# Variances of the second half of the tokens moved to ScalarE inside the query stage, with three sums moved

## The chip, the cores and the metric

The kernel runs on one core of a Trainium2 chip. A core has engines that run beside each other, each with its own in-order queue of instructions: TensorE (PE, matrix products into the eight PSUM banks), VectorE (DVE), ScalarE (ACT), GpSimd (POOL) and SyncE (SP), whose queue here only issues DMAs. Sixteen DMA engines move data between HBM and the on-chip SBUF. The metric is the device time of one execution in microseconds (us), as the median over several runs: 1160.79 us before the change (three runs, 1159.8 to 1162.68).

## What is computed

One transformer block in float32 on 16 sequences of 128 tokens with 1024 features each:

```python
x = x + xattn(_layernorm(x), ctx, ctx, w_q, w_k, w_v, w_out, mask)   # 32 query heads, 8 key/value groups
x = x + ffn(_layernorm(x), w12, b12, w3, b3)                         # (silu(x1) * x2) @ w3.T + b3

def _layernorm(x, axis=-1, eps=1e-05):
    m = jnp.mean(x, axis=axis, keepdims=True)
    v = jnp.var(x, axis=axis, keepdims=True)
    return (x - m) / jnp.sqrt(v + eps)
```

In the attention, `query = q @ w_q.T`, the scores are `query . key / sqrt(32)`, masked, put through a softmax and multiplied with the values. The change concerns the first layer norm only, and in it only the per-token variance.

## The kernel before

**How the first layer norm is folded away.** Queries are linear in the normalised x. The mean is removed from the weights instead of the tokens (`centre`, L442), so the query product runs on raw x. The factor 1/sqrt(var + eps) of each token is applied later, to the scores, as the per-partition number `rstd` of the instruction at L760. It is kept in `mr[T][:, 1, t]`: T = 0 for the sequences 0 to 7 (the first half) and T = 1 for 8 to 15. These numbers must be there before the first score row of the half is scaled, and for nothing else.

**How the variances are made.** For the first half `q_squares` (L622) does it on ScalarE inside the query stage: one pass over the 128x1024 tile `xs` sums it (L626), a tiny one makes minus the mean (L627), one more sums the squared deviations (L628). After the eighth sequence a GpSimd instruction divides by 1024 and `inv_std` (L213) turns eight variances into eight factors: seven tiny instructions on GpSimd and ScalarE. For the second half `q_stats` (L617) does it on VectorE with `mean_var` (L205): two `bn_stats` of 128x512, one `bn_aggr`, one copy of two numbers, for each of eight sequences. It is called from `hook` in `seven_round` (L727), along with the load of the tile, while keys and values of the second half are made.

**Products by seven.** Large matrix products are done with Strassen-like schemes (`seven`, L272): seven block products in place of eight, with sums of input blocks on the left and right made beforehand and sums of results made afterwards. The query product has two levels: outer products (g, i) with i from 1 to 7 for two halves g of the weights are the 14 entries of `Q_STEPS`, and each step runs seven inner products in the order 1, 5, 6, 7, 2, 3, 4. One inner product is four matrix passes, one step 28 passes, about 12 us. In a step, product 1 fills a PSUM bank, ScalarE copies it out (`p1`, L284), VectorE adds `u1` (L287) and `u3` (L290), and products 2, 3 and 4 go on accumulating into the banks of 1, 5 and 7. So product 3 waits until `u3` has read its bank.

**What the steps read.** Left sums of weights (`QI`, `q_inner_left`, L542) are made on GpSimd, four per step. Right sums of x come in two layers: outer sums (`q_outer_right`, L488), made mostly on GpSimd, in place, in tiles named `xq` and `Y`; inner sums (`q_inner_right`, L501), always on VectorE, in tiles `Y_T` (`Y7_T6` is inner sum 6 of outer product 7).

**What sets the order.** `q_at((n, j), ...)` puts a function into a plan that is called right after inner product number j of step n (`q_follow`). In steps 0 to 9 every engine's queue is written out in this order by hand. `q_plans` (L633) holds the plan. Steps 10 to 13, the seven-product rounds for keys and values of the second half (`seven_round(1, k)`) and the first output round run as filler between the attention instructions of the first eight sequences; TensorE's order is by hand there, and a scheduler orders the other engines at build time by the position of the code and the readiness of operands. The filler's left sums for keys (`sums_left7(1, 0)`, L693) are eight GpSimd subtractions and additions; `ctx_sum` (L695) makes right sums of the context on VectorE or GpSimd.

**Buffers.** Nearly all large tiles come from one pool of 44 units of 512 KB (`NUNIT`). A tile that is allocated takes a unit that became free, and its first writer waits for the last users of that unit. Loads are issued from the one SP queue in program order; a load that waits for its unit holds up everything behind it.

**Attention.** `scores` (L743) does, for one sequence and half of the heads, 16 score products, then VectorE scales and masks (L760) and finds the maximum (L763), ScalarE does the exponentials (L769), VectorE a reciprocal (L775), GpSimd the scaling (L778). The four score banks become free only when the exponentials have read them. `turn_V` (L422) transposes values on TensorE into a bank, `flip` (L781) transposes probabilities.

Of the kernel before, what the change touches and what calls it, by code (L numbers as in the profile page):

```python
# [13 lines left out]
AF = mybir.ActivationFunctionType  # L14
ALU = mybir.AluOpType
# [5 lines left out]
D = 1024  # L21
# [10 lines left out]
NT = B // 2  # L32
# [96 lines left out]
def xattn_ffn_kernel(  # L129
# [33 lines left out]
    nc = tc.nc  # L163
# [11 lines left out]
    def temp(shape, name):  # L175
        return temps.tile([P, *shape], F32, tag="tmp", name=name)
# [14 lines left out]
    def load(src, shape, name, eng=nc.sync):  # L191
        t = unit(shape, name)
        eng.dma_start(t, src)
        return t
# [10 lines left out]
    def mean_var(xt, dst, name):  # L205
        st = small.tile([P, 2, nc.vector.BN_STATS_DIM], F32, tag="st", name=f"st_{name}")
        for h in range(2):
            nc.vector.bn_stats(st[:, h, :], xt[:, ts(h, 512)])
        mv = small.tile([P, 2], F32, tag="mv", name=f"mv_{name}")
        nc.vector.bn_aggr(mv, st)  # L210
        nc.vector.tensor_copy(dst, mv)

    def inv_std(mr, name):  # L213

        n = mr.shape[2]
        v, t = (small.tile([P, NT], F32, tag=f"inv_std{i}", name=f"is{i}_{name}", bufs=2)[:, :n] for i in range(2))
        y = mr[:, 1, :]
        nc.gpsimd.tensor_scalar(v, y, EPS, None, ALU.add)
        nc.scalar.activation(t, v, AF.Ln)
        nc.scalar.activation(y, t, AF.Exp, scale=-0.5)  # L220
        nc.gpsimd.tensor_mul(t, y, y)
        nc.gpsimd.tensor_mul(t, t, v)
        nc.gpsimd.tensor_scalar(t, t, -0.5, 1.5, ALU.mult, ALU.add)
        nc.gpsimd.tensor_mul(y, y, t)
# [177 lines left out]
    mr = [const.tile([P, 2, NT], F32, tag=f"mr{T}", name=f"mr_{T}") for T in range(2)]  # L402
    later, xs = [], {}

    def soon(n, gen):

        later.append([n, gen])

    def tick():
        for item in list(later):  # L410
            item[0] -= 1
            if item[0] <= 0:
                later.remove(item)
                stream.work.appendleft(item[1])

    def load_xs(t):
        xs[t] = load(x[t], [D], f"xs_{t}")

    def stats(t):
        mean_var(xs.pop(t), mr[t // NT][:, :, t % NT], f"a{t}")  # L420

    def turn_V(T, c, r, t):  # L422

        pt = bank(f"vt_{T}_{c}_{r}").rearrange("p (t k) -> p t k", t=4)
        for i in range(4):
            nc.tensor.transpose(pt[:, i, :], t[:, ts(i, S)], ident)  # L426
            yield 0.17
        if (T, c) not in V:
            V[T, c] = unit([4, KV], f"V_{T}_{c}")
        nc.scalar.copy(V[T, c][:, :, ts(r, P)], pt)  # L430

    def key_home(T, c, r):
        if (T, c) not in KT:
            KT[T, c] = unit([GH, 512], f"K_{T}_{c}")
        return KT[T, c][:, r, :]
# [36 lines left out]
    def q_at(n, j, fn, *args):  # L472
        qplan.setdefault((n, j), []).append((fn, args))
# [140 lines left out]
            *((INNER,) if n < AHEAD else ((1, 6, 5, 7, 2, 3, 4), nc.vector.tensor_copy)),  # L614
        )

    def q_stats(t):  # L617
        stats(t)
        if t % NT == NT - 1:
            inv_std(mr[t // NT], f"a{t // NT}")  # L620

    def q_squares(t):  # L622

        xt = xs.pop(t)
        less = mr[0][:, 0, t : t + 1]
        nc.scalar.activation(xt, xt, AF.Identity, accum_out=less)  # L626
        nc.scalar.mul(less, less, -1.0 / D)  # L627
        nc.scalar.activation(xt, xt, AF.Square, bias=less, accum_out=mr[0][:, 1, t : t + 1])  # L628
        if t == NT - 1:
            nc.gpsimd.tensor_scalar(mr[0][:, 1, :], mr[0][:, 1, :], 1.0 / D, None, ALU.mult)  # L630
            inv_std(mr[0], "a0")

    def q_plans():  # L633
        for n, (g, i) in enumerate(Q_STEPS):
            if i > 2:
                q_at(n - 2, 3, q_load_left, g, i)
            for e, k in enumerate((1, 5, 6, 7, 3)):
                q_at(n - 1, 3 + e if n else min(5 + e // 2, 7), q_inner_left, g, i, k)
            if i in (1, 2, 5, 3):
                q_at(n - 1, 6 if n else 7, q_hold, g, i)  # L640
            if i == 1:
                q_at(g - 1, 7, q_keep_left, g, 4)
                q_at(g - 1, 7, q_outer_left, g)
                q_at(g, 7, q_keep_left, g, 3, 6)
                q_at(g + 1, 2, q_keep_left, g, 5, 7)
                q_at(n + 1, 2, q_store, g, i, "U")
            if i == 2:
                q_at(n + 1, 2, q_gather, g, 2, "U")
                q_at(n + 2, 3, q_final, g, 2, 0, 0)
            if i == 6:  # L650
                q_at(n - 2, 4, q_fetch, g, "U")
                q_at(n + 1, 2, q_store, g, "u", "V")
            if i == 7:
                q_at(n + 1, 2, q_store, g, "u", "W")
            if i == 4:
                q_at(n, 7, q_stay, g, "u", 1)
            if i == 5:
                q_at(n + 1, 3, q_gather, g, "V", 5)
                q_at(n + 1, 3, q_gather, g, "W", 5)
                q_at(n + 1, 4, q_given, g, "W", 1)  # L660
            if i == 3:
                q_at(*((n + 1, 3) if g == 0 else (n, 7)), q_gather, g, "V", 3)
                q_at(n, 7, q_given, g, "V", 0)
        for e, (K, C) in enumerate(((0, 0), (1, 0), (1, 1), (0, 1))):
            for f, (h, c) in enumerate(((0, 0), (0, 1), (1, 1), (1, 0))):
                when = ((-1, 3 + (f + 1) // 2), (0, 1 + f), (0, 5 + f // 2), (1, 2 + f))[e]
                q_at(*when, load_xq, K, C, h, c)
        for i, hcs, ks in (
            (1, [(-1, 5)] * 4, ((-1, 6), (-1, 6), (-1, 7), (0, 1))),
            (2, [(0, 6)] * 4, ((0, 7), (1, 1), (1, 2), (1, 7))),  # L670
            (5, [(2, 1), (2, 2), (2, 7), (3, 1)], ((8, 7), (9, 1), (9, 2), (9, 7))),
            (6, [(2, 7), (3, 1), (3, 3), (3, 3)], ((3, 5), (3, 6), (3, 7), (4, 1))),
            (7, [(4, 5), (5, 1), (5, 2), (5, 5)], ((5, 2), (5, 7), (6, 1), (6, 2))),
            (4, [(6, 5), (7, 1), (7, 2), (7, 5)], ((7, 2), (7, 7), (8, 1), (8, 2))),
            (3, [(4, 4)] * 4, ((4, 4), (5, 4), (8, 4), (8, 6))),
        ):
            for when, hc in zip(hcs, ((0, 0), (0, 1), (1, 1), (1, 0))):
                q_at(*when, q_outer_right, i, *hc)
            for when, k in zip(ks, (5, 6, 7, 4)):
                q_at(*when, q_inner_right, i, k)  # L680
        for t in range(NT):
            q_at(t + 1, 1, load_xs, t)
            q_at(t + 2, 2, q_squares, t)
        for m in (0, 1, 4, 5):
            q_at(8, 1 + m, q_home, 0, m)
        q_at(11, 3, load_left7, 1)
        for j, e in ((1, 0), (1, 5), (2, 1), (4, 3)):
            q_at(12, j, lambda e=e: ctx_work[1][e][1]())
        for when, i, e in (
            ((12, 6), 5, 0), ((12, 7), 5, 1), ((13, 2), 6, 0), ((13, 4), 6, 1), ((13, 5), 7, 0), ((13, 7), 7, 1),  # L690
        ):
            q_at(*when, ctx_sum, i, e)
        q_at(13, 3, sums_left7, 1, 0)  # L693

    def ctx_sum(i, e):  # L695

# [19 lines left out]
    def seven_round(T, k, R):  # L716
        def done(rc, s, ps):
            r, c = rc
            dst = temp([512], f"vT_{T}_{c}_{r}") if k else key_home(T, c, r)
            if s is None:  # L720
                nc.scalar.copy(dst, ps)
            else:
                nc.vector.tensor_add(dst, s, ps)
            if k:
                soon(3, turn_V(T, c, r, dst))

        def hook(j):  # L727
            tick()
            if (T, k, j) == (1, 0, 4):
                sums_left7(1, 1)  # L730
            if (T, k) == (1, 0) and j < 3:
                ctx_sum(4, j - 1)
            if T == 1 and j < 5:
                load_xs(NT + 4 * k + j - 1)
            if T == 1 and j > 2 and j < 7:
                q_stats(NT + 4 * k + j - 3)
            transition(T, k, j)

        yield from seven(left7.pop((T, k)), R, f"Q7_{T}_{k}", done, hook, (1, 2, 5, 6, 7, 3, 4))
# [249 lines left out]
    with tc.manual_schedule(engines={ENGINES.PE, ENGINES.DVE}):  # L989
        q_plans()  # L990
        Feed(ctx_work[0][:6], 100)
        sums_left7(0, 0, 1)
        stream.add(in_turn(seven_round(0, 0, ctx_R[0]), seven_round(0, 1, ctx_R[0]), 1))
        stream.finish()
# [4 lines left out]
    for T in range(2):  # L999
# [8 lines left out]
        for i in range(NT * GH):  # L1008
            t, gh = T * NT + i // GH, i % GH
# [333 lines left out]
    for t in range(8, B):  # L1343
        n, j = divmod(t - 8, 2)
# [68 lines left out]
```

## Time and profile before

The profile is that of one execution, by the hardware profiler.

| what | value |
|---|---|
| median of three runs | 1160.79 us |
| the profiled execution's own time | 1162.42 us |
| its span (first to last instruction) | 1160.6 us |
| mean granted TensorE clock | 0.997 of full |
| busy: PE / DVE / ACT / POOL | 98% / 73% / 34% / 56% of the span |
| one 512 KB load of an x tile (`xs`), issue to landing | 3.9 / 6.8 / 11.1 us (least, median, most of 16) |
| query stage, steps 0 to 9 | about 60 to 182 us |
| attention, first eight sequences | about 182 to 345 us |

How to read it: busy time says which engine has no slack; here that is TensorE. What it loses is then found as its idle stretches, each of which the profile gives with the instruction that ended it ("idle before <- releaser"), and in the granted clock, which is a share of full speed. Idle time of any other engine matters only where it ends in one of these stretches. Line numbers are those of the kernel before; in the kernel after, the lines from L422 on are 3 lower, those of `q_squares` 8 and then 7 lower, those from L695 on 5 lower, and those from L743 on 9 lower.

### The profile page before, as it was taken

To read this page: it belongs to the slowest core of one execution; us is meant where nothing else is said; L and a number is where in the kernel's file an instruction comes from. 1 tells how busy PE (TensorE), PEld (TensorE's weight loads), DVE (VectorE), ACT (ScalarE), POOL (GpSimd) and SP (SyncE) were. 2 spreads that over 40 slices of the span, in tenths; PEclk is the share of its full clock that TensorE was granted. 3 is DMA by queue.
4 is the path that set the end of the run, shared out by engine and by line. 5 is a ranking of instruction groups with operands and counts; after the bars stand their busy time and mean duration, and the time that the engine had idled before them with its cause. 6 is when DMAs were issued, how large, how long until landed. Compare 5 with 4: busy or idle time off the path is not lost.

```text
span 1160.6 us, 13625 instructions
## 1 busy us (share of the span) xinstructions
PE 1141.1 (98%) x4232; PEld 534.2 (46%) x4232; DVE 848.8 (73%) x1179; ACT 395.4 (34%) x1429; POOL 653.0 (56%) x591
## 2 busy tenths in 40 slices
PE   9999999999989999999999999999999999999998
PEld 4444444445445554545454544444444444444443
DVE  4577988798977778778546456757777887979772
ACT  1222223657557576666361321210011022111211
POOL 5669935786567456547533359822523342648465
PEclk9999999999989999999999999999999999999999
DMA  9699674954254330332584889858734878282511
GB/s 364 251 368 348 227 265 144 211 154 153 91 200 181 128 128 37 128 128 91 200 306 165 315 334 326 237 199 259 176 121 159 212 197 272 91 270 82 173 73 73
DMA packets 70233, 227.42 MB, mean 196 GB/s; under 512 B 7824, under 2 KB 7824, under 8 KB 70160
## 3 DMA queue, kind: packets, MB, share of 16 engines
q1 hardware_dynamic: 62672, 199.81, 46.7%
q0 software_dynamic: 6624, 24.12, 11.2%
q10 hardware_dynamic: 864, 2.62, 0.6%
q8 instruction: 34, 0.56, 0.2%
q14 instruction: 39, 0.32, 0.1%
HBM read 139.49 MB, written 79.69 MB: 189 GB/s over the span
## 4 chain that ended last, share of the span: by engine, by line
PE 91%; DVE 4%; ACT 2%; issue 1%; DMA 1%; POOL 1%; SPq 0%; ACTq 0%; POOLq 0%; DVEq 0%
PE F_b L199 28%; PE Q_b L199 21%; PE O_b L199 15%; PE G_b L199 15%; PE pt L784 4%; PE s L751 3%; PE o L799 2%; ACT p L769 2%; PE xt L899 1%; DVE ctx_T L700 1%; DVE s L760 0%; DVE xnT L1066 0%; DVE Y_T L509 0%; DMA xnr<-xn_dram 0%; PE vt L426 0%
## 5 line engine op out<-in xcount | busy, mean ns | idle before, releaser
L769 ACT ACTIVATE p<-s,nmax 128x128 f32<-128x128 f32 x512 | 181.8, 406 | 125.7 <-DVE nmax L763 114.8
L778 POOL TENSOR_TENSOR p<-p,inv 128x512 f32<-128x512 f32 x128 | 136.4, 1098 | 138.4 <-DVE inv L775 121.1
L199 PE MATMUL F_b<-X_T,L 128*128 128x512 f32 x304 | 135.7, 592 | 0.0
L769 ACT ACTIVATION_READ_ACCUMULATOR p<-s,nmax 128x1 f32 x512 | 125.5, 245 | 0.0
L199 PE MATMUL G_b<-w_R,A_L 128*128 128x512 f32 x256 | 114.5, 592 | 0.0
L760 DVE SCALAR_TENSOR_TENSOR s<-s,mr,drop 128x512 f32<-128x512 f32 x128 | 90.3, 750 | 28.8 <-PE s L751 28.6
L784 PEld LDWEIGHTS pt<-ident,p 128*128 128x128 f32 x512 | 63.6, 142 | 70.0 <-issue 63.5
L199 PEld LDWEIGHTS F_b<-X_T,L 128*128 128x128 f32 x304 | 57.4, 190 | 70.8 <-issue 68.6
L763 DVE TENSOR_REDUCE nmax<-s 128x4 f32<-128x512 f32 x128 | 81.7, 679 | 0.0
L284 ACT COPY F_p<-F_b 128x512 f32<-128x512 f32 x28 | 16.4, 586 | 188.3 <-PE F_b L199 188.3
L784 PE MATMUL pt<-ident,p 128*128 128x128 f32 x512 | 77.3, 274 | 1.5 <-issue 1.5
L303 POOL TENSOR_TENSOR x<-x,G_n 128x512 f32<-128x512 f32 x36 | 52.8, 1491 | 46.3 <-DVE G_n L366 29.4
L384 ACT COPY G_c<-G_b 128x512 f32<-128x512 f32 x52 | 30.5, 586 | 140.7 <-PE G_b L199 137.3
L199 PEld LDWEIGHTS G_b<-w_R,A_L 128*128 128x128 f32 x256 | 48.6, 190 | 61.3 <-issue 59.3
L1176 DVE TENSOR_TENSOR M<-F_u,F_b 128x512 f32<-128x512 f32 x57 | 39.0, 685 | 46.3 <-PE F_b L199 42.8
L303 POOL TENSOR_TENSOR x<-x,G_c 128x512 f32<-128x512 f32 x36 | 54.8, 1538 | 31.9 <-DMA x<-x_dram 13.0
L199 PE MATMUL Q_b<-Y_T,QI 128*128 128x512 f32 x136 | 62.4, 594 | 1.9 <-DVE Y_T L509 1.9
L199 PE MATMUL O_b<-wo_T,O_S 128*128 128x512 f32 x128 | 63.3, 603 | 0.0
L199 PE MATMUL O_b<-wo,O_S 128*128 128x512 f32 x128 | 62.5, 602 | 0.0
L199 PE MATMUL F_b<-xnT,L 128*128 128x512 f32 x128 | 60.9, 593 | 0.0
L199 PE MATMUL O_b<-wo,OTr 128*128 128x512 f32 x112 | 56.0, 603 | 0.0
L287 DVE TENSOR_TENSOR F_u<-F_b,F_p 128x512 f32<-128x512 f32 x28 | 19.3, 691 | 45.2 <-PE F_b L199 41.5
(244 smaller groups left out, 2265.9 us busy)
## 6 DMA issues: line engine op xcount, KB each, us to landing
w<-in_w_dram SPq DMA_DIRECT2D x36, 512.0 KB, 6.3
xq<-in_xT_dram SPq DMA_DIRECT2D x16, 512.0 KB, 9.8
xs<-in_x_dram SPq DMA_DIRECT2D x16, 512.0 KB, 6.8
xp<-in_x_dram SPq DMA_DIRECT2D x16, 512.0 KB, 6.6
x_dram<-xp SPq DMA_DIRECT2D x16, 512.0 KB, 2.8
xn_dram<-xn SPq DMA_DIRECT2D x16, 512.0 KB, 2.9
xnr<-xn_dram SPq DMA_DIRECT2D x16, 512.0 KB, 5.7
h<-hT_dram SPq DMA_DIRECT2D x16, 512.0 KB, 6.0
```

The source lines that it names most:

```text
L199: nc.tensor.matmul(ps, lhsT, rhs, start=start and i == 0, stop=stop and i == len(pairs) - 1, skip_group_check=True,)
L287: nc.vector.tensor_add(u1, banks[6], p1)
L303: (eng.tensor_add if op == "+" else eng.tensor_sub)(out, a, b)
L384: nc.scalar.copy(t, ps)
L751: nc.tensor.matmul(ps[gl][:, j, :], QT[T, gh * HPG + j][rows, c, toks], KT[T, c][rows, gh, toks], start=True, stop=True,)
L760: nc.vector.scalar_tensor_tensor(s, s, rstd, drop.unsqueeze(1).to_broadcast([P, HPG, S]), ALU.mult, ALU.add,)
L763: nc.vector.tensor_reduce(nmax[:, e], s, AX.X, ALU.max, negate=True)
L769: nc.scalar.activation(p[:, j, :], ps[gl][:, j, :], AF.Exp, bias=nmax[:, e, j : j + 1], accum_out=total[:, e, j : j + 1],)
L778: nc.gpsimd.tensor_mul(p, p, inv[:, e].unsqueeze(2).to_broadcast([P, HPG, S]))
L784: nc.tensor.transpose(pt[:, j, :], p[:, j, :], ident)
L799: nc.tensor.matmul(o[ds(gl * DH, DH), :, :], V[T, c][:, i, ts(gh * GL + gl, DH)], pTs[gl], start=True, stop=True,)
L1176: nc.vector.tensor_add(dst, s, ps)
```

## The change

It does four things.

1. The eight second-half variances leave VectorE and the key/value rounds: `stats` and `q_stats` are gone, and `q_squares` now serves both halves. The loads of the tiles xs_8 to xs_15 are issued in steps 3 to 6, after inner products 3 and 5, and the three ScalarE instructions for each come in steps 4 to 7, after products 4 and 6. The eighth is followed in step 7 by the GpSimd and ScalarE instructions of `inv_std`.
2. In step 5, inner sum 6 of outer product 7 (`Y7_T6`) is made after product 4 and not after 7.
3. The inner sums of outer product 3 (`Y3_T6`, the one in place, and `Y3_T4`) move from (5, 4), (8, 4), (8, 6) to (8, 3), (8, 5), (9, 4).
4. `sums_left7(1, 0)` is called at (12, 2) and not at (13, 3), which is ahead of the context sums.

```diff
--- before.py
+++ after.py
@@ -416,9 +416,6 @@
     def load_xs(t):
         xs[t] = load(x[t], [D], f"xs_{t}")
 
-    def stats(t):
-        mean_var(xs.pop(t), mr[t // NT][:, :, t % NT], f"a{t}")
-
     def turn_V(T, c, r, t):
 
         pt = bank(f"vt_{T}_{c}_{r}").rearrange("p (t k) -> p t k", t=4)
@@ -614,21 +611,17 @@
             *((INNER,) if n < AHEAD else ((1, 6, 5, 7, 2, 3, 4), nc.vector.tensor_copy)),
         )
 
-    def q_stats(t):
-        stats(t)
-        if t % NT == NT - 1:
-            inv_std(mr[t // NT], f"a{t // NT}")
-
     def q_squares(t):
 
         xt = xs.pop(t)
-        less = mr[0][:, 0, t : t + 1]
+        T, e = divmod(t, NT)
+        less = mr[T][:, 0, e : e + 1]
         nc.scalar.activation(xt, xt, AF.Identity, accum_out=less)
         nc.scalar.mul(less, less, -1.0 / D)
-        nc.scalar.activation(xt, xt, AF.Square, bias=less, accum_out=mr[0][:, 1, t : t + 1])
-        if t == NT - 1:
-            nc.gpsimd.tensor_scalar(mr[0][:, 1, :], mr[0][:, 1, :], 1.0 / D, None, ALU.mult)
-            inv_std(mr[0], "a0")
+        nc.scalar.activation(xt, xt, AF.Square, bias=less, accum_out=mr[T][:, 1, e : e + 1])
+        if e == NT - 1:
+            nc.gpsimd.tensor_scalar(mr[T][:, 1, :], mr[T][:, 1, :], 1.0 / D, None, ALU.mult)
+            inv_std(mr[T], f"a{T}")
 
     def q_plans():
         for n, (g, i) in enumerate(Q_STEPS):
@@ -670,9 +663,9 @@
             (2, [(0, 6)] * 4, ((0, 7), (1, 1), (1, 2), (1, 7))),
             (5, [(2, 1), (2, 2), (2, 7), (3, 1)], ((8, 7), (9, 1), (9, 2), (9, 7))),
             (6, [(2, 7), (3, 1), (3, 3), (3, 3)], ((3, 5), (3, 6), (3, 7), (4, 1))),
-            (7, [(4, 5), (5, 1), (5, 2), (5, 5)], ((5, 2), (5, 7), (6, 1), (6, 2))),
+            (7, [(4, 5), (5, 1), (5, 2), (5, 5)], ((5, 2), (5, 4), (6, 1), (6, 2))),
             (4, [(6, 5), (7, 1), (7, 2), (7, 5)], ((7, 2), (7, 7), (8, 1), (8, 2))),
-            (3, [(4, 4)] * 4, ((4, 4), (5, 4), (8, 4), (8, 6))),
+            (3, [(4, 4)] * 4, ((4, 4), (8, 3), (8, 5), (9, 4))),
         ):
             for when, hc in zip(hcs, ((0, 0), (0, 1), (1, 1), (1, 0))):
                 q_at(*when, q_outer_right, i, *hc)
@@ -681,6 +674,8 @@
         for t in range(NT):
             q_at(t + 1, 1, load_xs, t)
             q_at(t + 2, 2, q_squares, t)
+            q_at(3 + t // 2, 3 + t % 2 * 2, load_xs, NT + t)
+            q_at(4 + t // 2, 4 + t % 2 * 2, q_squares, NT + t)
         for m in (0, 1, 4, 5):
             q_at(8, 1 + m, q_home, 0, m)
         q_at(11, 3, load_left7, 1)
@@ -690,7 +685,7 @@
             ((12, 6), 5, 0), ((12, 7), 5, 1), ((13, 2), 6, 0), ((13, 4), 6, 1), ((13, 5), 7, 0), ((13, 7), 7, 1),
         ):
             q_at(*when, ctx_sum, i, e)
-        q_at(13, 3, sums_left7, 1, 0)
+        q_at(12, 2, sums_left7, 1, 0)
 
     def ctx_sum(i, e):
 
@@ -730,10 +725,6 @@
                 sums_left7(1, 1)
             if (T, k) == (1, 0) and j < 3:
                 ctx_sum(4, j - 1)
-            if T == 1 and j < 5:
-                load_xs(NT + 4 * k + j - 1)
-            if T == 1 and j > 2 and j < 7:
-                q_stats(NT + 4 * k + j - 3)
             transition(T, k, j)
 
         yield from seven(left7.pop((T, k)), R, f"Q7_{T}_{k}", done, hook, (1, 2, 5, 6, 7, 3, 4))
```

## The prediction

> **What bounds the kernel now.** I read the busy shares first, then TensorE's waits and the granted clock, and then the stretches in which these waits lie, engine by engine. The first line says that TensorE is the bound and that nothing else is near it.
>
> ```profile
> PE 1141.1 (98%) x4232; PEld 534.2 (46%) x4232; DVE 848.8 (73%) x1179; ACT 395.4 (34%) x1429; POOL 653.0 (56%) x591
> ```
>
> So only what opens or closes a gap on TensorE counts. Its list of waits has two large entries.
>
> ```profile
> PE vt L426 <- ACT p L769: 5.3, 1, 5.3
> PE Q_b L199 <- DVE Y_T L509: 1.9, 1, 1.9
> ```
>
> The timeline puts the 1.91 us at 135.0 to 136.9, step 6, where product 6 waits for the inner sum `Y7_T6`, and the 5.34 us at 318.5 to 323.9, where a transpose of values wants a bank that a score tile holds. Why the score tile is late stands in VectorE's timeline: between the reciprocal at 313 and the scaling of the scores at 320.2 stand half a variance, two sums of the output weights, the copy of a variance and a quarter of the next.
>
> ```profile
> 313.12 1.24 DVE L208 BATCH_NORM_STATS2 st_a<-xs 128x6 f32<-128x512 f32 x2
> 314.27 1.22 DVE L242 TENSOR_TENSOR wo_T<-wo,wo_T 128x1024 f32<-128x1024 f32 x1
> ...
> 317.39 2.31 DVE L211 COPY mr<-mv_a 128x2 f32<-128x2 f32 x1
> 319.62 0.68 DVE L208 BATCH_NORM_STATS2 st_a<-xs 128x6 f32<-128x512 f32 x1
> 320.22 1.40 DVE L760 SCALAR_TENSOR_TENSOR s<-s,mr,drop 128x512 f32<-128x512 f32 x2
> ```
>
> The gap also costs clock. In windows of 1 us the clock column (after the POOL column) falls to half at about 321.2 and is back at 328.0:
>
> ```profile
> 321.00:322.00 1.00, 0.00 (x0) 0.00 (x0) 1.00 (x2) 0.00 (x0) 0.98 (x1) 0.59 0.00 0
> 327.00:328.00 1.00, 1.00 (x4) 0.69 (x3) 0.90 (x3) 1.00 (x9) 0.91 (x2) 0.50 1.09 336
> ```
>
> TensorE works again from 323.9, so it runs 4.1 us at half speed and loses 2.1 us more. After the gap of 1.9 us the clock stayed at 1.00.
>
> The query stage, where the work goes to, is full in another way. GpSimd is busy for 95% of 80 to 120 us, and the DMA engines (share before the last column) are saturated until 119:
>
> ```profile
> 112.00:116.00 4.00, 4.00 (x11) 1.73 (x10) 2.89 (x4) 0.45 (x2) 4.00 (x4) 1.00 1.05 259
> ...
> 120.00:124.00 4.00, 4.00 (x11) 1.74 (x10) 3.93 (x6) 2.61 (x5) 3.92 (x3) 1.00 0.27 109
> ```
>
> **The change, part by part.** Its sum is made against the profiled execution's own 1162.42 us, which lies 1.6 us above the median of the runs; 1.6 is taken off at the end.
>
> *1. ScalarE.* A square costs 1.06 for the sum, 0.20 for the mean and 1.15 for the squares, with two accumulator reads of 0.19; from the first start (85.76) to the last end (88.42) that is 2.66 us. Steps 4 to 7 then hold three, 8.0 us, and the copy of product 1, 0.59, in a step of 12.0. The row shows ScalarE idle for 8.87 us ahead of this copy, and two more squares take 5.3 of them. The division by 1024 and `inv_std` are seven instructions of 0.2 to 0.8 us, about 2 us once.
>
> ```profile
> 121.33 0.59 ACT L284 COPY Q_p<-Q_b 128x512 f32<-128x512 f32 x1 [8.87 <-PE Q_b L199]
> ```
>
> I cost it at nothing. The cover is the 3.4 us that are left; if a tile lands later than that, the copy waits behind its squares, with `u1` and `u3` on VectorE and products 2 and 3 behind it.
>
> *2. VectorE in attention.* Sixteen `bn_stats` of 0.67, eight aggregates of 0.2 and eight copies go, some 14 us. All but one stretch is beside other work, as no wait of TensorE ends on them. In the stretch, 1.15 + 0.12 + 2.23 + 0.59 = 4.1 us stood ahead of the scaling, so it moves up from 320.2 to 316.1, and the gap shrinks from 5.34 to 1.2. That is one end. The other comes from GpSimd: in the new order its two subtractions on output weights (5.63 us for two) stand one ahead of the second pair of `p` and one behind it, so the first runs when VectorE makes its two `wo_T`. What that does, two rows of the same VectorE operation show, one beside a GpSimd subtraction of this size and one with GpSimd idle:
>
> ```profile
> 116.06 3.36 DVE L509 TENSOR_TENSOR Y_T<-xq,xq 128x1024 f32<-128x1024 f32 x1
> ...
> 159.13 1.22 DVE L509 TENSOR_TENSOR Y_T<-xq,Y_T 128x1024 f32<-128x1024 f32 x1
> ```
>
> Two times 2.1 us is the worst, and I take 1.3, since the `wo_T` of 314.27 and 315.53 had already 1.22 and 1.94: a gain of 2.8 (between 0 and 4.1). The gap of 2.5 then lies between the one that kept the clock (1.9) and the one that lost it; I take the whole 2.1 as gained (0 to 2.1).
>
> *3. The `Y7_T6` that TensorE waits for.* It takes the place of `Y3_T6` in VectorE's queue (127.88, where it was 133.41) and so the 1.9 us go. Late next is the in-place sum `xq` of outer product 7, which product 7 of step 6 reads: 1.8 us behind product 6, and behind five result additions and 1.7 us of its own. In the profile it ends at 138.4 just as the product starts.
>
> *4. The eight loads, and the store in front of GpSimd.* This is the term that speaks against the change. In the changed program's order the first weight sum for step 5 (`QI6_1`) has another buffer: it waits for the landing of the store `Q_dram_0_0`, where before it waited for product 4 of step 3, done at 107.6. GpSimd's rows there:
>
> ```profile
> 109.16 1.06 POOL L303 TENSOR_TENSOR QI<-QL 128x256 f32<-128x256 f32 x1
> 110.30 1.60 POOL L303 TENSOR_TENSOR QI<-QI,QL 128x256 f32<-128x256 f32 x1
> 111.86 2.36 POOL L499 TENSOR_TENSOR xq<-xq,xq 128x1024 f32<-128x1024 f32 x1
> ...
> 115.55 6.10 POOL L499 TENSOR_TENSOR xq<-xq,xq 128x1024 f32<-128x1024 f32 x2
> ```
>
> The store was issued at 105.72 in SP's queue and landed 8.0 us later.
>
> ```profile
> 105.72 4.06 SPq L580 DMA_DIRECT2D Q_dram<-QM  x2
> ```
>
> Now xs_8, xs_9 and xs_3 stand ahead of it; xs_3 waits for its own buffer until 107.6, so the store goes out at 108.05 and lands at 116.1 if nothing else changes. But the DMA engines are full, and xs_8 and xs_9 are 0.5 MB each in front: 1.27 us each at the 410 GB/s of the fullest slices, and twice that while GpSimd's accumulating DMAs take half. So the landing is between 116.1 and 121, and I take 118.2, as the accumulating DMAs are in flight throughout. SP's other late issues (1 to 5 us) have caught up by 109.5.
>
> Queued behind the waiting sum on GpSimd are three more of `QI6_1`, two outer sums of product 7 and, a little further, two more and the weight sums of steps 6 and 7; GpSimd has no slack to catch up before 155. From the landing to the second outer sum `xq` the six instructions take 7.6 us alone (four of 0.73, two of 2.36) and took 9.2 in the profile: it is done between 123.7 and 130.2, taken 126.6. VectorE waits there with `Y7_T5`: 1.2 to 3.4 us, taken 3.4, because GpSimd begins its next outer sum at once. Behind it in VectorE's queue stand `u1` and `u3` of step 5, 0.7 each, and TensorE's product 3, due at 127.99, waits for `u3`: 126.6 + 3.4 + 1.4 = 131.4. The new gap is 3.4 us, between nothing and 7.0.
>
> VectorE then carries the delay into step 6: `Y7_T6` (1.2 to 3.4), five additions (0.7 each, the last two gated by TensorE) and the in-place `xq` (1.2 to 3.4) end some 4 to 9 us after `u3` did at its earliest; against product 7 of step 6, itself 3.4 later, a second gap of 2.4 us (0 to 3.5).
>
> The Trainium skill ("TensorE: Matmul & The Clock Gate", Part 1) says that an idle window of about 3.4 us, in a window that runs freely, halves the clock. By it the new gap may or may not trigger, as the phase falls; no run here shows one of this size. A gap of 1.9 kept the clock and one of 5.3 lost it, with 2.1 us paid. For the gap of 3.4, which lies in the middle, I take 1.7 (0 to 3).
>
> *5. The rest.* `Y3_T6`, 1.7 us, joins step 8 where VectorE's rows show idle time of 0.2 to 1.0 us at a time, and `Y3_T4`, 1.2, joins step 9 ahead of the first scores. TensorE waits 0.9 us for `u1` at 193.05 behind those scores; I add 0.6 (0 to 1.4). The keys' eight left sums are 5.8 us of GpSimd work, moved past two DMAs of results and six `p`; no flip waits for these. At 252.5 VectorE's `ctx_T` took 4.0 us beside four `p` in a row, and TensorE lost 0.9 after it. With the left sums gone from there the `p` come in pairs: a gain of 0.5 (0 to 0.9). SP's loads in the key/value rounds only go.
>
> Sum: -2.8 - 2.1 (attention) - 1.9 + 3.4 + 2.4 + 1.7 (steps 5 and 6) + 0.6 - 0.5 = +0.8. That is 1163.2 against the profiled execution, or **1161.6 us** as a median: the query stage takes back what the attention gives.
>
> **The rivals.**
>
> *A. The store is not late; faster.* If it lands at 116 or before, GpSimd's sum is there by 123.7, VectorE is not held, and gap, second gap and clock cost nothing. What speaks for it: the queue's depth at 108 is the least certain number here, as SP issued nothing from 100.9 to 107.6. Then -2.8 - 2.1 - 1.9 - 0.5 + 0.6 = -6.7: 1154.1. With my middle values the gap opens from a landing of 114.8, with the low ones from 117.8, so A needs the low ones.
>
> *B. The store lands at 120 or later; slower.* Everything in step 5 then moves with it, microsecond for microsecond: a gap of 5.4 in place of 3.4, and the clock surely lost (3.0), the second gap at its 3.5. For it: 1.05 DMA share through the whole stretch. Against it: the share falls at 119. Sum +0.8 + 2.0 + 1.3 + 1.1 = +5.2: 1166.0. It decides from a landing of about 119.
>
> *C. The attention gap stays.* If GpSimd holds both `wo_T` for the whole 2.1 us, the gap stays at about 5 and the clock falls again: +0.8 + 2.8 + 2.1 = +5.7, 1166.5. Against it: two rows of 1.22 and 1.94 in the same place.
>
> *D. ScalarE is late.* If xs_11 or xs_13 lands over 3.4 us late, the copy of product 1 waits, 1 us for each, in up to four steps: +4 on top.
>
> **How the numbers follow.** The sum's own case has 0.45; A 0.20; B 0.22; C 0.09; D 0.04. A change of 0.3% (3.5 us) is about what a measurement of this kernel can tell from none. The first case stays within it; A is faster; B, C and D are slower: 0.20, 0.45, 0.35. The range goes from A with some of its gap back, 1155.5, to B with some of C, 1168.
>
> **What would show it.** TensorE's waits after: none at `vt` over 3 us, none for `Y7_T6`, a new one in step 5 (product 3, on `u3`) of some 3.4 us and one in step 6 on `xq` of some 2.4. GpSimd is idle from 109 to about 118, ended by a DMA. The clock column has no half-speed slices at 321 and may have some at 132. ScalarE's copy of product 1 has its old place in each step. I am wrong if GpSimd starts that sum by 116, if the `vt` gap stays above 4, or if TensorE waits on ScalarE in steps 5 to 8.

## The result and the profile after

The changed kernel takes 1166.46 us (median of five runs, 1165.01 to 1167.45) against 1160.33 for the kernel before: a ratio of 1.0048, 95% interval 1.0036 to 1.0061. It is 6.1 us slower. The profiled execution has a span of 1164.4 us and a time of its own of 1166.17. TensorE is still the bound and everything else still has slack, so the answer lies in TensorE's waits. The first line of the page, and then the list of TensorE's waits (us in total, how often, the longest):

```profile
PE 1140.3 (98%) x4232; PEld 532.6 (46%) x4232; DVE 838.3 (72%) x1147; ACT 415.0 (36%) x1469; POOL 651.4 (56%) x592
```

```profile
PE Q_b L199 <- POOL QI L303: 4.5, 2, 4.1
PE vt L423 <- ACT p L760: 2.4, 1, 2.4
PE pt L775 <- ACT p L760: 1.6, 1, 1.6
...
PE Q_b L199 <- DVE xq L506: 1.2, 1, 1.2
...
PE Q_b L199 <- DVE Q_p L284: 0.9, 1, 0.9
```

The `vt` entry fell from 5.3 to 2.4 and the wait for `Y7_T6` is gone, as forecast. New are 4.5 us for a GpSimd sum, 1.6 us at a flip of probabilities (`pt`) and 1.2 us for `xq`. The next view is TensorE's own timeline in steps 5 and 6, where the brackets at the end of a line hold the idle time before the instruction and what ended it:

```profile
122.67 1.98 PE L199 MATMUL Q_b<-Y_T,QI 128*128 128x512 f32 x4 [0.43 <-POOL QI L303]
...
130.48 3.56 PE L199 MATMUL Q_b<-Y,QI 128*128 128x512 f32 x4 [4.11 <-POOL QI L303]
...
142.10 1.95 PE L199 MATMUL Q_b<-xq,QI 128*128 128x512 f32 x4 [1.20 <-DVE xq L506]
```

The pass at 130.48 is product 3 of step 5. What it waited for begins on GpSimd, 13 us earlier:

```profile
106.12 0.86 POOL L570 DMA_DIRECT2D QM<-QU_dram  x1 [0.63 <-DVE QM L603]
117.75 0.72 POOL L303 TENSOR_TENSOR QI<-QL 128x256 f32<-128x256 f32 x1 [10.76 <-DMA Q_dram<-QM]
...
123.27 4.66 POOL L496 TENSOR_TENSOR xq<-xq,xq 128x1024 f32<-128x1024 f32 x2
127.89 1.70 POOL L303 TENSOR_TENSOR QI<-QL 128x256 f32<-128x256 f32 x1
129.67 0.73 POOL L303 TENSOR_TENSOR QI<-QI,QL 128x256 f32<-128x256 f32 x1
```

GpSimd stands still for 10.76 us, until the store `Q_dram_0_0` has landed (117.58). VectorE waits for the second of its outer sums, and makes `Y7_T5` beside the third; `u1` and `u3` come behind it, and `u3` ends at 130.34, 0.1 us ahead of the GpSimd sum that the profile names:

```profile
125.66 3.35 DVE L506 TENSOR_TENSOR Y_T<-xq,xq 128x1024 f32<-128x1024 f32 x1 [6.64 <-POOL xq L496]
128.93 0.68 DVE L287 TENSOR_TENSOR Q_u<-Q_b,Q_p 128x512 f32<-128x512 f32 x1
129.65 0.69 DVE L290 TENSOR_TENSOR Q_u<-Q_b,Q_u 128x512 f32<-128x512 f32 x1
```

The gap costs clock as well. Windows of 1 us (TensorE's busy time is the second number, the clock the third from the right) show half speed from 130.3 to 133.7, and again from 328.3 to 331.7, behind what is left of the `vt` gap:

```profile
131.00:132.00 1.00, 1.00 (x2) 0.33 (x1) 1.00 (x1) 0.00 (x0) 1.00 (x1) 0.50 1.07 320
132.00:133.00 1.00, 1.00 (x2) 0.33 (x1) 1.00 (x1) 0.00 (x0) 1.00 (x2) 0.50 0.97 389
...
329.00:330.00 1.00, 1.00 (x5) 0.85 (x4) 0.90 (x2) 1.00 (x7) 0.88 (x1) 0.50 0.00 0
```

**Where the 6 us lie.** TensorE's order is the same in both kernels, so the start of each matrix pass in one profile can be taken from its start in the other; where the difference jumps, time was lost or won. One warning: all passes after the first 11 us come 2.5 us earlier in the profile after, since that execution's clock reached full speed sooner (the first 8 passes took 3.67 us, and 6.49 in the profile before). This is chance and no part of the change. "Scale of before" below means 2.5 us added. From there on the jumps are:

| stretch | forecast | measured |
|---|---|---|
| step 5: gaps of 0.43 and 4.11, and the clock behind | +3.4 and +1.7 | +6.7 |
| step 6: `Y7_T6` | -1.9 | -2.1 |
| step 6: `xq` | +2.4 | +1.3 |
| step 8 | 0 | +0.5 |
| first scores | +0.6 | +0.8 |
| flips and scores, 237 to 243 on before's scale | 0 | +3.1 |
| 257 on before's scale | -0.5 | -1.2 |
| `vt`: the gap / its clock | -2.8 / -2.1 | -3.1 / -0.3 |
| rest | 0 | +0.5 |
| sum | +0.8 | +6.2 |

The row of 257 can't be credited to part 4, though I first took it for its gain: runs without part 4 show the same -1.1 to -1.2 there (below: parts 2 and 3 alone, `best_product`). The third large row, +3.1, has its cause on VectorE and GpSimd:

```profile
234.08 5.46 DVE L695 TENSOR_TENSOR ctx_T<-ctx,ctx 128x1024 f32<-128x1024 f32 x1
239.46 0.68 DVE L603 TENSOR_TENSOR QM<-Q_u,Q_b 128x512 f32<-128x512 f32 x1
240.06 1.41 DVE L751 SCALAR_TENSOR_TENSOR s<-s,mr,drop 128x512 f32<-128x512 f32 x2
```

```profile
233.89 2.52 POOL L769 TENSOR_TENSOR p<-p,inv 128x512 f32<-128x512 f32 x2
235.89 1.20 POOL L303 TENSOR_TENSOR QI<-QI,QL 128x256 f32<-128x256 f32 x1
236.57 1.20 POOL L303 TENSOR_TENSOR QI<-QL 128x256 f32<-128x256 f32 x1
237.26 1.19 POOL L303 TENSOR_TENSOR QI<-QL,QI 128x256 f32<-128x256 f32 x1
```

The first context sum takes 5.46 us, where the same instruction took 1.22 in the profile before. It is issued 0.2 us after GpSimd began the last five instructions of an unbroken run and ends 1.1 us after the last of them (238.45), which is about its own length: it was shut out for all five. The scaling of the scores stands behind it, the scores hold their PSUM banks 3 us longer, and a flip waits 1.6 us for one; 0.8 us more of idle time follow, for which the profile names no releaser. In the kernel before, the sum came at the same time as the last `p` of this group, and there it was the `p` that waited (2.12 us, where the one ahead of it took 1.04) while the sum took its 1.22:

```profile
229.37 1.22 DVE L700 TENSOR_TENSOR ctx_T<-ctx,ctx 128x1024 f32<-128x1024 f32 x1
```

```profile
228.37 3.12 POOL L778 TENSOR_TENSOR p<-p,inv 128x512 f32<-128x512 f32 x2 [0.49 <-DVE inv L775]
```

### The profile page after: what moved, and what is told of

It is laid out like the page before. It is cut to its first block, busy times and chain, and to the rows that moved or that the text cites. A ratio compares the mean times of both kernels' runs of the same rounds, so it can differ in the third digit from the quotient of the medians.

```text
span 1164.4 us, 13637 instructions
## 1 busy us (share of the span) xinstructions
PE 1140.3 (98%) x4232; PEld 532.6 (46%) x4232; DVE 838.3 (72%) x1147; ACT 415.0 (36%) x1469; POOL 651.4 (56%) x592
## 4 chain that ended last, share of the span: by engine, by line
PE 85%; DVE 6%; DMA 3%; issue 2%; ACT 2%; POOL 1%; SPq 0%; ACTq 0%; DVEq 0%; POOLq 0%
PE F_b L199 28%; PE Q_b L199 16%; PE O_b L199 15%; PE G_b L199 15%; PE pt L775 4%; PE s L742 3%; PE o L790 2%; ACT p L760 2%; DMA Q_dram<-QM 1%; DVE Y_T L506 1%; DVE s L751 1%; PE xt L890 1%; DVE nmax L754 1%; DMA xs<-in_x_dram 1%; DVE QUr L597 1%
## 5 line engine op out<-in xcount | busy, mean ns | idle before, releaser
L769 POOL TENSOR_TENSOR p<-p,inv 128x512 f32<-128x512 f32 x128 | 139.0, 1124 | 137.5 <-DVE inv L766 119.1
```

The costliest lines, as they stand in the source:

```text
L769: nc.gpsimd.tensor_mul(p, p, inv[:, e].unsqueeze(2).to_broadcast([P, HPG, S]))
```

## The experiments

The theory: two losses, each from one part. Part 1 makes GpSimd wait for a store that lands late; part 4 pushes GpSimd's work onto VectorE's context sum. The rivals are written in each expectation. All runs were timed in five rounds beside the kernel before.

**The parts alone.**

Part 1 alone is the changed kernel with the other three taken back:

```diff
-            (7, [(4, 5), (5, 1), (5, 2), (5, 5)], ((5, 2), (5, 4), (6, 1), (6, 2))),
+            (7, [(4, 5), (5, 1), (5, 2), (5, 5)], ((5, 2), (5, 7), (6, 1), (6, 2))),
...
-            (3, [(4, 4)] * 4, ((4, 4), (8, 3), (8, 5), (9, 4))),
+            (3, [(4, 4)] * 4, ((4, 4), (5, 4), (8, 4), (8, 6))),
...
-        q_at(12, 2, sums_left7, 1, 0)
+        q_at(13, 3, sums_left7, 1, 0)
```

> Part 1 alone (second-half variances on ScalarE, with their loads in steps 3 to 6); the three other parts are as before. Theory: GpSimd's first sum for step 5 waits for the landing of the store Q_dram_0_0, as in the changed kernel: GpSimd idle for about 10 us from 107, a gap of 3 to 6 us in step 5, half a clock window (1.7 us) behind it, and a gap of 1 to 4 us at Y7_T6 or xq in step 6; the vt gap is 2 to 3 us. Then +6.7 (step 5 with its clock) + 0 to 2 (step 6) - 3.4 (attention): 1163 to 1166 us, slower than before by 3 to 5.5. Rival 1 (the price comes from the moved sums of outer products 7 and 3): GpSimd waits but TensorE does not, and the run is at about 1157. Rival 2 (it comes from the left sums and the score rows): the loss in step 5 is under 2 us and the run at 1157 to 1159.

1166.98 us, ratio 1.0062 (1.0049 to 1.0075): +6.6, and 1 us above the range that I gave. GpSimd's wait is the same to the hundredth, and the gap within a hundredth:

```profile
119.05 0.72 POOL L303 TENSOR_TENSOR QI<-QL 128x256 f32<-128x256 f32 x1 [10.76 <-DMA Q_dram<-QM]
```

```profile
131.78 3.39 PE L199 MATMUL Q_b<-Y,QI 128*128 128x512 f32 x4 [4.12 <-POOL QI L303]
143.52 2.37 PE L199 MATMUL Q_b<-Y_T,QI 128*128 128x512 f32 x4 [3.19 <-DVE Y_T L506]
```

The excess is the second row. Without parts 2 and 3 the wait for `Y7_T6` is still there, and the late step 5 makes 3.2 us of 1.9; that halved the clock a second time, from 144.9 to 148.3. Both rivals fall: part 1 alone opens the gap.

Parts 2 and 3 alone are the reverse of these first two pairs of lines, on the kernel before:

```diff
-            (7, [(4, 5), (5, 1), (5, 2), (5, 5)], ((5, 2), (5, 7), (6, 1), (6, 2))),
+            (7, [(4, 5), (5, 1), (5, 2), (5, 5)], ((5, 2), (5, 4), (6, 1), (6, 2))),
...
-            (3, [(4, 4)] * 4, ((4, 4), (5, 4), (8, 4), (8, 6))),
+            (3, [(4, 4)] * 4, ((4, 4), (8, 3), (8, 5), (9, 4))),
```

> Parts 2 and 3 alone (inner sum 6 of outer product 7 three products up, inner sums of outer product 3 into steps 8 and 9). Theory: the wait of 1.9 us for Y7_T6 in step 6 goes (-2.0), and the sums in steps 8 and 9 cost what the changed kernel lost there, 0.5 in step 8 and 0.8 at the copy of product 1 in step 10 (+1.3): 1159.5 us, between 1158.5 and 1160.5; no gap in step 5. Rival (these sums open the gap in step 5): TensorE waits 3 us or more in step 5 and the run is at 1163 or above.

1158.84 us, 0.9986 (0.9977 to 0.9995): -1.5, inside the range, with no gap in step 5. TensorE's waits have no entry for `Y_T` any more, and 0.2 for `xq`. The costs that I had put on these sums do not appear. The wait in step 8 (0.26 us) is in the profile of part 1 alone; the 0.8 in step 10 is in neither of the two, and why it comes with both together stays open.

Part 4 alone, on the kernel before:

```diff
-        q_at(13, 3, sums_left7, 1, 0)
+        q_at(12, 2, sums_left7, 1, 0)
```

> Part 4 alone (left sums for keys ahead of the context sums). Theory: the eight GpSimd instructions push GpSimd's p and QI3_1 behind the place where VectorE makes the first context sum ctx_1_T5_0; that sum takes 4 to 5.5 us in place of 1.2, the score rows behind it are late, and TensorE waits about 1.6 us for a bank between 236 and 246: +1.9 us, 1162.2 (1161 to 1163). Rival, my prediction's value: GpSimd has room, the late p come in pairs, -0.5: 1159.8. Second rival: the long context sum in the changed kernel came from the missing variances, not from the left sums; then it takes 1.2 to 1.8 us here and the run is within 0.5 us of before.

1164.49 us, 1.0035 (1.0022 to 1.0047): +4.1, above my range, and far from my prediction's -0.5. VectorE's sum and TensorE's wait:

```profile
228.95 5.70 DVE L700 TENSOR_TENSOR ctx_T<-ctx,ctx 128x1024 f32<-128x1024 f32 x1
```

```profile
238.88 0.63 PE L784 MATMUL pt<-ident,p 128*128 128x128 f32 x4 [1.84 <-ACT p L769]
240.28 1.10 PE L199 MATMUL Q_b<-Y_T,QI 128*128 128x512 f32 x2 [0.77 <-issue]
```

This rules out the second rival: the variances are still on VectorE here, and the sum is as long. In this profile the differences of the starts make +3.3 by 243 and +3.2 at the end, and the two waits cost no clock. Why the median is 0.9 us worse stays open. Clock lost at these waits is not the reason: the granted clock is 0.997 in all six runs, as in this profile, and one more half-speed window, 1.7 us of 1163, would have made it 0.996.

The three runs add up to +9.2 us (6.6 - 1.5 + 4.1), where the whole change lost 6.1. So parts 2 and 3 were worth some 4.6 us inside the change, if part 4 keeps its price there, and 1.5 by themselves: they also clear the 3.2 us that part 1 makes of the wait in step 6, and its clock.

**The store or the full DMA engines?** Part 1 does two things at once: it puts two loads ahead of the store, and it gives GpSimd's sum the store's buffer. To part them I moved each load of the changed kernel by one inner product. The bytes in the crowded stretch are the same, but the units fall otherwise, and the buffer of `QI6_1` is that of `xs_2`:

```diff
-            q_at(3 + t // 2, 3 + t % 2 * 2, load_xs, NT + t)
+            q_at(3 + t // 2, 4 + t % 2 * 2, load_xs, NT + t)
```

> The changed kernel with the loads of xs_8 to xs_15 one inner product later (after products 4 and 6 of steps 3 to 6). The same bytes are moved in the same saturated stretch, but the units fall otherwise: GpSimd's first sum for step 5 waits for ScalarE's square of xs_2 (done at about 110) and no longer for the store Q_dram_0_0, which is as late as before. Theory (the wait for the store is the cause): GpSimd starts this sum at about 110 in place of 117.7, the gap of 4.1 us in step 5, the half clock after it and the gap of 1.2 in step 6 go: 1166.5 - 6.7 - 1.3 = 1158.5 us, between 1157 and 1160.5. Rival (the saturated DMA engines delay the step by themselves, through the load of the weights QL_1_6 or other tiles): the gap stays at 3 us or more and the run at 1163 to 1166.5.

1158.95 us, 0.9983 (0.9974 to 0.9991), with part 4 still in. The store is as late as ever: issued at 105.80, landed at 117.83 (105.55 and 117.58 in the changed kernel). But nothing on GpSimd waits for it:

```profile
110.22 0.72 POOL L303 TENSOR_TENSOR QI<-QL 128x256 f32<-128x256 f32 x1 [3.07 <-ACT xs L621]
111.02 0.73 POOL L303 TENSOR_TENSOR QI<-QI,QL 128x256 f32<-128x256 f32 x1
111.70 2.36 POOL L496 TENSOR_TENSOR xq<-xq,xq 128x1024 f32<-128x1024 f32 x1
```

TensorE's timeline marks no idle time in steps 5 and 6. So the loss of step 5 is the buffer's wait for the store; full DMA engines alone cost TensorE nothing here. The `pt` wait of 1.6 us remains, and in this execution it cost clock, from 236.8 to 240.2.

**Part 4 in another place.** On the kernel before, the left sums go to (11, 7), where GpSimd had been idle:

```diff
-        q_at(13, 3, sums_left7, 1, 0)
+        q_at(11, 7, sums_left7, 1, 0)
```

> The kernel before with the left sums for keys called at (11, 7): four of the eight GpSimd instructions then stand ahead of p_1_0_0, in a stretch where the profile of before has GpSimd idle from 211 to 214.3, and four behind p_1_0_1; the idle time from 221 to 225 takes up the delay before p_1_1_0. Theory (part 4 loses because GpSimd's p and QI3_1 are pushed onto VectorE's first context sum): the sum ctx_1_T5_0 takes 1.2 to 2 us again, no wait over 0.5 us at the flips between 234 and 242, and what the earlier sums gain at 250 to 260 (some -1.2 in both runs that have part 4) stays: 1159.5 us, 1158.5 to 1160.8. Rival (left sums ahead of the context sums cost by their order, wherever the room is): the context sum is long again and the run is at 1162.5 or above.

1160.37 us, 0.9994 (0.9986 to 1.0003): the loss is gone. The context sum is short again:

```profile
228.43 1.21 DVE L700 TENSOR_TENSOR ctx_T<-ctx,ctx 128x1024 f32<-128x1024 f32 x1
```

So it is not the order of left sums and context sums that costs, but where GpSimd's run of instructions comes to lie. I then put both remedies into the changed kernel: left sums at (11, 7) and the loads one inner product later, and in a second kernel the loads a whole step later and the squares with them:

```diff
-        q_at(12, 2, sums_left7, 1, 0)
+        q_at(11, 7, sums_left7, 1, 0)
...
-            q_at(3 + t // 2, 3 + t % 2 * 2, load_xs, NT + t)
-            q_at(4 + t // 2, 4 + t % 2 * 2, q_squares, NT + t)
+            q_at(4 + t // 2, 3 + t % 2 * 2, load_xs, NT + t)
+            q_at(5 + t // 2, 4 + t % 2 * 2, q_squares, NT + t)
```

> The changed kernel with the loads one inner product later (as in the run loads_1prod_later, 1158.95) and the left sums at (11, 7). Theory: the two losses of the change are independent; what part 4 cost (2.1 us of start times, 4.1 in the medians) comes off: 1156 us, between 1154.5 and 1157.5. TensorE's largest wait is the one at vt, 2.4 us. Rival: with the score rows moved, the collision comes back at another context sum, and the run stays at 1158 to 1159.

> As combo_product, but the loads of xs_8 to xs_15 in steps 4 to 7 (after products 3 and 5) and their squares in steps 5 to 8. None of them stands ahead of the store Q_dram_0_0, and GpSimd's first sum for step 5 waits for product 4 of step 3 as in the kernel before. Theory: GpSimd starts it at 107 on the changed kernel's time scale and no wait over 0.5 us is left in steps 5 and 6: 1156 us, 1154.5 to 1157.5, the same as combo_product within 1 us. Rival (the landings in steps 6 to 8 become late in their turn): a wait of 1 us or more for a sum of outer product 4 or for a Q result, and 1158 to 1161.

1156.16 us, 0.9968 (0.9953 to 0.9983), and 1156.14 us, 0.9972 (0.9956 to 0.9987). The medians are as expected, but the runs fall into two groups: 8 of 12 at 1154.3 to 1157.1 and 4 at 1160.6 to 1162.0 in the first kernel, 7 at 1154.7 to 1156.4 and 5 at 1160.6 to 1163.2 in the second. The granted clock goes with the groups: 0.995 to 0.997 in every run of the upper ones, 0.998 to 1.000 in every run of the lower ones. Both profiles are of the upper group, and both show the rival of the first expectation: the collision is back, at the next two context sums. The rows are those of the first kernel:

```profile
234.95 3.81 DVE L695 TENSOR_TENSOR ctx_T<-ctx,ctx 128x1024 f32<-128x1024 f32 x1
238.68 0.68 DVE L780 COPY pT<-pt 128x512 f32<-128x512 f32 x1
239.28 2.98 DVE L695 TENSOR_TENSOR ctx_T<-ctx,ctx_T 128x1024 f32<-128x1024 f32 x1
```

```profile
243.59 1.01 PE L742 MATMUL s<-K,Q 32*128 32x128 f32 x9 [3.68 <-DVE pT L780]
```

They took 1.22 and 1.46 in `left_11_7`, the run before. TensorE's wait of 3.68 us halved the clock behind it in both profiles (for 6.8 and 3.4 us). GpSimd's `p` and VectorE's sum begin there within half a microsecond of each other, so I read the two groups as this contest going one way or the other; there is no profile of a lower-group execution, so that half is not shown.

**Parts 2 and 3 each alone.**

> Part 2 alone (Y7_T6 three products up). Theory: the wait of 1.9 us in step 6 goes, the in-place xq behind it is just in time, and nothing else moves: 1158.4 us, 1157.5 to 1159.3. Rival: Y3_T6, which part 3 would have taken out of this place, still stands there and pushes the sums of step 5: a new wait of 1 us or more in step 5 or 6 and 1159.5 to 1160.5.

> Part 3 alone (inner sums of outer product 3 into steps 8 and 9). Part 2 alone measured no gain, since the in-place xq became late by 1.2 us; parts 2 and 3 together gained 1.5. Theory: VectorE's 1.7 us for Y3_T6 in step 5 is what made either late; without it Y7_T6 in its old place is ready 1.7 us earlier, the wait of 1.9 us shrinks to 0.2 and xq is in time: 1159.3 us, 1158.5 to 1160.3. Rival: Y7_T6 waits for its own place behind the additions of step 5, the 1.9 us stay, and the run is at 1160.5 or above.

1161.12 us, 1.0000 (0.9992 to 1.0009), and 1161.05 us, 0.9995 (0.9986 to 1.0004). I missed them by 2.7 and 1.8 us: each alone is worth nothing that the medians show. Each removes the wait for `Y7_T6` and gets one for `xq` in its place, as the rival for part 2 had it (a new wait of 1 us or more); in the list of waits of part 2 alone, and of part 3 alone:

```profile
PE Q_b L199 <- DVE xq L509: 1.2, 1, 1.2
```

```profile
PE Q_b L199 <- DVE xq L509: 1.3, 1, 1.3
```

My reading is that VectorE is short of some 1.5 us in steps 5 and 6 for whichever sum comes last. Part 2 brings `Y7_T6` forward by making `xq` late, part 3 takes 1.7 us of work away, and only both together clear the two products.

**What the parts are worth without the losses.** Parts 1 to 3 with the loads moved and the left sums where the kernel before had them, with the loads one inner product later and one step later:

> Parts 1 to 3 with the loads one inner product later; the left sums for keys stay where they were before (no part 4). Theory: what part 4 cost alone (+3.3 us of TensorE's waits between 236 and 246, 4.1 in the medians) comes off the 1158.95 of loads_1prod_later, and with GpSimd's old order at the context sums the second, slower group of times that the two runs with the left sums at (11, 7) had (1160.6 to 1163) does not appear: 1155.2 us, 1154 to 1156.5, all runs within 1.5 us of the median. Rival (the two groups come from part 1, not from the place of the left sums): again some runs 4 to 6 us above the others.

> As best_product with the loads one step later (steps 4 to 7, squares in 5 to 8). Theory: as no wait in the query stage remains in either, the same time within 1 us: 1155.2 us, 1154 to 1156.5. Rival: a late landing in steps 6 to 8 shows up here, 1157 or more.

1155.36 us, 0.9950 (0.9938 to 0.9963), and 1156.29 us, 0.9956 (0.9942 to 0.9969). The runs of the first lie between 1154.4 and 1156.9, those of the second between 1153.9 and 1157.7, and there are no two groups. So part 1 is sound once its loads are moved: parts 1 to 3 are 5 to 6 us faster than before, where part 1 with its first loads was 6.6 us slower, and parts 2 and 3 alone gave 1.5. The second kernel has a wait of 1.1 us for `xq` left, against my theory that none remains; the medians still differ by less than the 1 us that I allowed.

The last run takes up what was left of the `vt` gap, on `best_product`. VectorE's two sums of output weights stood ahead of the scores; in the profile after:

```profile
319.52 4.25 DVE L242 TENSOR_TENSOR wo_T<-wo,wo_T 128x1024 f32<-128x1024 f32 x2
323.70 1.41 DVE L751 SCALAR_TENSOR_TENSOR s<-s,mr,drop 128x512 f32<-128x512 f32 x2
```

```diff
-            feeds["wo"].give(2)
+            feeds["wo"].give(2 if j != 3 else 0)
```

> best_product, and the two sums wo_T6 of the output weights, which VectorE makes ahead of the scores of sequence 5 at about 319.5 (2.27 and 2.06 us beside a GpSimd subtraction), one inner product later, behind those scores. Theory: what is left of the vt gap is these two sums; the scaling of the scores then starts when TensorE has made them (at 322.0 on the changed kernel's time scale, 1.7 us earlier), the gap of 2.4 us shrinks to 0.7 and the clock no longer halves there: best_product - 1.7 - 0 to 1.7, 1153 us, 1151.5 to 1154.5. Rival: the gap stays because another instruction holds the bank: the same time as best_product.

1153.98 us, 0.9935 (0.9923 to 0.9948), the fastest kernel here, 7.3 us below the kernel before as timed beside it and 1.4 below `best_product`, where I had expected 1.7 or more. The scaling now waits for TensorE and not for VectorE, and of the gap 0.8 is left:

```profile
312.74 1.42 DVE L751 SCALAR_TENSOR_TENSOR s<-s,mr,drop 128x512 f32<-128x512 f32 x2 [2.44 <-PE s L742]
```

```profile
PE vt L423 <- ACT p L760: 0.8, 1, 0.8
```

## Why the prediction was right and wrong

The forecast was 1161.6 us, a change of less than 0.3%, to which I had given 0.45; it came out at 1166.46, slower by 0.5%, inside the range (1155.5 to 1168.0) but near its upper end, on the side to which I had given 0.35. The range held; the case that I thought most likely did not come. Two terms of the sum had the wrong size (the pace of the loads in 5, the clock in attention in 3) and one had the wrong sign (the left sums in 6). By steps:

1. *ScalarE* (costed at nothing): right. The copy of product 1 comes at its old place in step 5 (118.85, 121.35 on before's scale, against 121.33). No TensorE wait names ScalarE's squares.
2. *The gap in attention* (-2.8, to 2.5 us): right, 2.43. The two `wo_T` stood beside a GpSimd subtraction and a `p`, as argued from the new order, and took 2.27 and 2.06.
3. *The clock in attention* (-2.1, "the whole"): wrong, -0.3. I placed 2.5 "between the one that kept the clock (1.9) and the one that lost it" and then took the whole gain instead of weighing it. In the profile after, 2.43 us were enough to halve it. In `best_product`'s profile a gap of the same length kept it. It is a matter of phase, as told at the end.
4. *The wait for `Y7_T6`* (-1.9) *and `xq` as next*: right in kind. -2.1, and 1.2 us for `xq`, where I had 2.4.
5. *The store* (landing 118.2 on before's scale): the mechanism was right, the size was not. It was issued at 105.55, which is 108.05 on that scale, exactly as forecast, and landed at 120.1: 12.0 us in flight, not the 10.2 that I took nor the 8.0 of before. The step at fault is the pace of the loads ahead: on before's scale `QL_1_6` lands at 104.0 in both, then `xs_8`, `xs_9` and `xs_3` at 107.7, 114.0 and 117.9, where `xs_3` alone had landed at 111.3. Two loads more moved it by 3.3 us each; I had 1.27 each, and twice that as the worst. So the gap was 4.5 and not 3.4. By the landing this is rival B's case, past its threshold of 119. That B's 1166.0 is so near is partly luck: B had 5.4 + 3.5 + 3.0 for the two gaps and the clock, the trace has 4.5 + 1.2 + 1.7, and what made up the difference are the next point and point 3.
6. *The left sums* (-0.5, "no flip waits for these"): the step that failed worst, +3.1 in the profile and +4.1 us alone. I looked only for who waits for the moved instructions, and for a gain where they had been. Who stood behind them I named (six `p`) and did not follow: about 1 us later against VectorE, `p` and `QI3_1` meet its context sum. The rows that I used for `wo_T`, 3.36 beside a GpSimd subtraction against 1.22, were in hand for exactly this; and the one long row I did quote, `ctx_T` with 4.0 us beside four `p`, I read as a thing that the change would remove, not as a thing that it could make elsewhere.

Two smaller terms: step 8, where I had nothing, cost 0.5. For the first scores I had 0.6 and the trace has 0.8, but at another place: the wait of 0.9 us at 193.05 is for `u3` (L290) and not for `u1`, as I had read it, and it stayed as it was; what grew is the wait for the copy of product 1, from 0.2 to 0.9 us.

Rival A (a store that is not late) fell with point 5, C (the gap stays at 5) with point 2, D (late loads hold ScalarE) with point 1. No rival held the collision, which cost about half as much as the store in the profile after.

## What to carry to other kernels

A tile that takes over a buffer also takes over the last user's lateness: when a change adds loads, look at which buffers shift, and for each engine that now waits for a store, ask when that store lands with the new traffic in front of it. When work is moved on GpSimd, follow everything that stands behind it to the next instruction of VectorE that reads two SBUF tiles; if that falls into an unbroken run of GpSimd instructions, it can cost the rest of the run and not one instruction of it. And a part that measures nothing alone can be worth its full price beside another: `Y7_T6` and `xq` needed both of their sums moved.

## What the runs showed of the hardware

**The clock falls on less than a full idle window.** The changes of the granted clock lie on a grid of 3.413 us, whose phase differs from run to run. I laid this grid over TensorE's idle time in the profiles of all fourteen kernels. Every window at full speed with 1.92 us idle or more was followed by half speed (15 windows, from 1.92 to 3.41), and every one with 1.84 us or less by full speed. At half speed less is enough to stay there: windows with 0.79, 1.28, 1.35, 1.66 and 2.70 us idle were followed by another at half speed, those with up to 0.51 by full speed; one exception, with no idle time, held most of the narrow score products. The windows at the start of an execution fit no such limit: one with 0.59 us idle stayed at half speed (parts 2 and 3 alone), and one with 0.69 went to full (`loads_1prod_later`). The Trainium skill ("TensorE: Matmul & The Clock Gate", Part 1) has the free-running window of about 3.4 us, and the grid agrees; it speaks of an idle window, and here a little over half of one was enough. So a gap of 2.43 us costs up to 1.7 us more when it lies in one window, as in the profile after, and nothing when the grid cuts it. In `best_product` the same gap, from 315.4 to 317.8, lies across a boundary at 316.4, and the windows of 1 us show full speed in it and behind it:

```profile
316.00:317.00 1.00, 0.00 (x0) 0.00 (x0) 1.00 (x3) 0.71 (x5) 1.00 (x1) 1.00 0.00 0
317.00:318.00 1.00, 0.16 (x1) 0.16 (x2) 1.00 (x2) 1.00 (x8) 0.45 (x1) 1.00 0.00 0
318.00:319.00 1.00, 1.00 (x6) 0.53 (x5) 1.00 (x3) 1.00 (x8) 0.00 (x0) 1.00 0.00 0
```

Full speed begins at 4.0 us in the profile after and at 10.6 in the profile before, which makes the 2.5 us above; I take some of the spread of 2 to 4 us between runs of one kernel to come from there. A price for clock is therefore a chance and not a sum.

**VectorE can be shut out for a run of GpSimd instructions, not only for one.** The Trainium skill ("SBUF — State Buffer", SBUF: two separate sides) says that a VectorE instruction with two SBUF inputs and a GpSimd instruction share a port pair, which the one that starts first holds to its end. The rows of the kernel before agree (1.22 and 2.12 in the pair above). In step 5 of the profile after, too, the sum at 125.66 waited for one GpSimd instruction (3.35 us), and the next one, in an unbroken run, waited for it (1.70 us in place of 0.72). But in all three profiles with part 4 in its new place the context sum waited for five GpSimd instructions in a row (5.46, 5.70 and 5.43 us). There the rows of GpSimd overlap, each 256-wide sum beginning 0.68 us after the last and taking 1.2, while at that place in the kernel before they took 0.73 with the same spacing. In all three the overlap begins at DMAs that GpSimd issues, some 13 us ahead, and GpSimd has no pause from there on. The overlap is not the whole story: in the kernel before, the `ctx_T` at 252.51 took 4.00 us beside three `p` that do not overlap (1.03 us each, 1.00 apart):

```profile
252.51 4.00 DVE L700 TENSOR_TENSOR ctx_T<-ctx,ctx_T 128x1024 f32<-128x1024 f32 x1
```

What lets VectorE in was not tried.
